# A layer norm moved from TensorE transposes to GpSimd with factors spread over DRAM, in a two-layer convolution and attention kernel

## The chip, the cores and the metric

The kernel runs on one core of a Trainium2 chip. The metric is the device time of one execution in microseconds. A time is given as the median of several executions; a profile is one execution, and its span is a few microseconds shorter than the time. The kernel before took 929.19 us.

Engines are named as in the profile: PE is TensorE's matmul, PEld its weight load, DVE VectorE, ACT ScalarE, POOL GpSimd, SP SyncE, which issues most DMAs.

## The reference, cut to what matters

Layer 0 normalises each pixel over its 128 channels, adds a depthwise 3x3 convolution, and attends inside 16x16 windows; layer 1 is linear attention and a recurrence over the tokens.

```python
def _layernorm2d(x, g, b):                    # x is (4, 128, 64, 64)
    mean = x.mean(axis=1, keepdims=True)      # over the 128 channels
    var = ((x - mean) ** 2).mean(axis=1, keepdims=True)
    return (x - mean) / jnp.sqrt(var + EPS) * g + b

y = _layernorm2d(x, ln_g, ln_b)
y = y + _cpe(y, cpe_w, cpe_b)                 # depthwise 3x3
q, k, v = 1x1 projections of y in 16x16 windows, 2 branches x 4 heads
o = softmax(q . 5x5 neighbours of k) applied to v     # zero padding counts in the sum
x = x + (Wo of o)
# layer 1: t = t + linear_attention(norm(t)); t = t + recurrence(norm(t))
```

## The kernel before

The image is cut into 16 bands of 16 rows, a band into 4 windows. The program is one long interleaving: while TensorE does window i's attention (six "gaps" a window), one step of `ahead` (norm and convolution of the next band) and one step of `behind` (layer 1 of the band before) are put into a gap. The program holds each engine of the list `ENGINES` to the order in which its instructions are written, so the place of a step decides what it waits behind. (The first window of a band takes steps of `ahead` in three of its gaps only, so a band has 3 + 3 x 6 = 21 of them.)

The norm needs sums over channels. The statistics are taken with tokens on the partitions, where one instruction sums over channels; the convolution wants channels on the partitions. So four pieces of 128 tokens are scaled on VectorE, turned by TensorE, and evicted by ScalarE into a padded image:

```python
def turn(g):
    j0, j1 = groups[g]
    rows = turned(xn.pop(g), 0, j1 - j0)[:, : (j1 - j0) * P]   # 4 PE transposes
    ...
    evict(y[:, 2 * j0 + 1 : k1, 1 : W + 1], rows[...])          # ACT, from PSUM
measure(0); yield; measure(1); yield; scale(0); yield
for g in range(len(groups)):
    turn(g); scale(g + 1); measure(g + 2); yield
...
def taps(y2, y, c0, width, each):
    for tap in range(9):
        src = y[:, dy : dy + WS, c0 + dx : c0 + dx + width]
        if tap == 0:
            nc.scalar.activation(y2, src, AF.Identity, bias=cpe_b, scale=cpe_w[:, 0:1])
        else:
            nc.vector.scalar_tensor_tensor(y2, src, cpe_w[:, tap : tap + 1], y2, ALU.mult, ALU.add)
        if tap % each == 0:
            yield
def convolve(n, half):             # half a band: two windows
    yield from taps(y2, y, half * 2 * WS, 2 * WS, 1 + half)
    nc.scalar.copy(y2w, y2)        # (views cut) the projections of two windows read y2w
```

A band has sixteen such taps on VectorE, eight for each half.

The sums of the softmax go ScalarE, DMA (`dc`), VectorE (inverses), DMA to DRAM (`rd`), DMA back to all partitions (`rden`), and GpSimd multiplies (`oT`). Layer 1's first matmuls of a band (line 471 before, 552 after) read `oT`; their starts serve below as the mile post of a band.

## Time and profile before

| | before |
|---|---|
| time, median | 929.19 us (928.76 to 930.86) |
| span of the profile | 925.6 us |
| mean granted clock | 0.981 |
| start to first line 471 | 77.57 us |
| first to second band | 50.16 us |
| 13 bands, from 127.73 to 779.47 us | 651.74 us, 50.13 each |
| last band to last product | 42.83 us |
| rest | 103.3 us |

The five stretches add up to the span. The row of the 13 steady bands is the one to watch; this is its line of busy times, with the columns that the prediction explains:

```profile
127.73:779.47 651.74, 648.91 (x8363) 495.55 (x8359) 550.74 (x1849) 406.12 (x739) 180.20 (x252) 1.00 0.19 55
```

TensorE is idle for 651.74 - 648.91 = 2.8 us in thirteen bands. Why that is so shows in how one half of the convolution is made (the timeline of the kernel before; columns: start, duration, engine, line, what, and in brackets the idle time before it, if any):

```profile
449.58 0.74 DVE L294 SCALAR_TENSOR_TENSOR y<-ypad,cpe_w,y 128x512 f32<-128x512 f32 x1
451.36 0.74 DVE L294 SCALAR_TENSOR_TENSOR y<-ypad,cpe_w,y 128x512 f32<-128x512 f32 x1
452.13 0.62 ACT L330 COPY y2w<-y 128x512 f32<-128x512 f32 x1
...
454.61 1.03 PE L343 MATMUL bank<-y2w,wqT 128*128 128x256 f32 x4
```

The eight taps of this half began at 437.73 us and came one or two at a time between VectorE's other work. The copy starts as the last tap ends, and the matmuls that read it start 2.5 us later: they do not wait. The list of waits (engine, line, the one waited for, us in total, times, longest) has the copies, and no matmul of line 343 behind a copy:

```profile
ACT y2w L330 <- DVE y L294: 17.5, 16, 5.8
```

### The profile page before, as it was taken

The numbers are of one execution on the slowest core, as the hardware profiler recorded it, in microseconds if no ns is written. First come the engines' busy times: TensorE is split into PE (matmuls) and PEld (weight loads), VectorE is DVE, ScalarE is ACT, GpSimd is POOL, SyncE is SP. The second block draws the span as 40 slices with busy tenths as digits, with TensorE's granted clock in tenths as the row PEclk, the third lists the DMA queues.
The fourth block names the chain that finished last, engine by engine and source line by source line (L and its number), as shares of the span: only waits on it lengthen the run. The fifth ranks groups of instructions, "written<-read, shape, count | busy, mean of one in ns | idle before, by whom it ended". The sixth has DMA issues, their size and how long they took to land.

```text
span 925.6 us, 26464 instructions
## 1 busy us (share of the span) xinstructions
PE 876.4 (95%) x10508; PEld 655.1 (71%) x10508; DVE 730.4 (79%) x2408; ACT 540.1 (58%) x1010; POOL 260.8 (28%) x358
## 2 busy tenths in 40 slices
PE   4978999999999999999999999999999999977894
PEld 3856777877777877777787777777777878665452
DVE  6464979888798878798888889787879887578684
ACT  3655656565756565665657575666666565623563
POOL 2122141423232232304132323323230412121195
PEclk9988999999999999999999999999999999989898
DMA  4112121122212121212112121212121111153254
GB/s 122 26 46 62 38 70 49 47 59 63 60 55 60 54 57 49 74 38 68 49 51 60 60 60 49 62 45 73 49 70 39 55 37 50 41 210 132 86 219 150
DMA packets 53189, 63.46 MB, mean 69 GB/s; under 512 B 22976, under 2 KB 33856, under 8 KB 52416
## 3 DMA queue, kind: packets, MB, share of 16 engines
q1 hardware_dynamic: 51616, 61.10, 21.1%
q8 instruction: 85, 1.39, 0.6%
q10 hardware_dynamic: 1440, 0.57, 0.2%
q14 instruction: 48, 0.39, 0.1%
HBM read 35.44 MB, written 17.30 MB: 57 GB/s over the span
## 4 chain that ended last, share of the span: by engine, by line
PE 61%; DVE 24%; ACT 5%; POOL 4%; issue 3%; DMA 2%; ACTq 0%; POOLq 0%; DVEq 0%; SPq 0%
PE bank L343 8%; DVE y L294 8%; PE bank L471 7%; PE bank L388 6%; PE bank L218 6%; PE bank L500 5%; PE bank L406 4%; PE bank L356 4%; PE bank L418 4%; PE bank L608 3%; DVE st L197 2%; PE z L834 2%; PE bank L579 2%; PE bank L543 2%; PE bank L581 2%
## 5 line engine op out<-in xcount | busy, mean ns | idle before, releaser
L294 DVE SCALAR_TENSOR_TENSOR y<-ypad,cpe_w,y 128x512 f32<-128x512 f32 x240 | 189.8, 791 | 17.1 <-ACT y L292 13.6
L397 ACT ACTIVATE es<-bank 128x512 f32<-128x512 f32 x256 | 132.2, 602 | 77.0 <-PE bank L388 77.0
L446 POOL TENSOR_TENSOR oT<-o_sb,rden 128x512 f32<-128x512 f32 x64 | 83.9, 1311 | 242.7 <-DMA rden<-rd 138.4
L201 POOL TENSOR_SCALAR rs<-mv 128x4 f32<-128x4 f32 (+2 forms) x100 | 25.1, 251 | 366.5 <-DVE mv L199 163.2
L209 DVE TENSOR_SCALAR xn<-x,mv,rs 128x128 f32<-128x128 f32 x256 | 89.9, 412 | 26.6 <-POOL rs L202 26.6
L202 POOL TENSOR_TENSOR rs<-rs,mhalf 128x4 f32<-128x4 f32 (+2 forms) x100 | 106.3, 1063 | 8.3
L388 PEld LDWEIGHTS bank<-q,k 32*128 32x128 f32 x3072 | 97.7, 189 | 7.5 <-ACT k L351 6.3
L388 PE MATMUL bank<-q,k 32*128 32x96 f32 (+1 forms) x3072 | 96.3, 270 | 1.1 <-ACT k L351 1.1
L418 PEld LDWEIGHTS bank<-es,v_sb 128*32 128x32 f32 x3072 | 56.6, 110 | 30.2 <-issue 20.2
L471 PE MATMUL bank<-woT,oT 128*128 128x128 f32 x512 | 68.0, 289 | 5.8 <-POOL oT L446 5.8
L471 PEld LDWEIGHTS bank<-woT,oT 128*128 128x128 f32 x512 | 64.8, 202 | 9.9 <-POOL oT L446 7.5
L500 PE MATMUL bank<-xl,awT 128*128 128x512 f32 x128 | 70.0, 630 | 0.0
L418 PE MATMUL bank<-es,v_sb 128*32 128x96 f32 (+1 forms) x3072 | 69.9, 239 | 0.0
L406 PE MATMUL bank<-es,ones 128*32 128x512 f32 x512 | 69.1, 612 | 0.0
L363 ACT COPY v_sb<-bank 128x512 f32<-128x512 f32 x64 | 37.6, 587 | 53.6 <-PE bank L356 44.6
L343 PE MATMUL bank<-y2w,wqT 128*128 128x256 f32 x256 | 67.3, 386 | 1.0 <-DVE y2w L294 1.0
L343 PE MATMUL bank<-y2w,wkT 128*128 128x256 f32 x256 | 66.7, 384 | 0.0
L356 PE MATMUL bank<-wvT,y2w 128*128 128x256 f32 x256 | 66.0, 380 | 0.0
L351 ACT COPY q<-bank 128x512 f32<-128x512 f32 x64 | 37.7, 588 | 42.2 <-PE bank L343 40.2
L351 ACT COPY k<-bank 128x512 f32<-128x512 f32 x64 | 37.4, 584 | 37.6 <-PE bank L343 37.5
L197 DVE BATCH_NORM_STATS2 st<-x 128x6 f32<-128x128 f32 x256 | 55.5, 280 | 1.1
L343 PEld LDWEIGHTS bank<-y2w,wqT 128*128 128x128 f32 x256 | 46.0, 195 | 13.0 <-issue 7.2
(118 smaller groups left out, 1713.7 us busy)
## 6 DMA issues: line engine op xcount, KB each, us to landing
rden<-rd SPq DMA_DIRECT2D x64, 256.0 KB
v_sb<-v_sb SPq DMA_DIRECT2D x128, 64.0 KB
resd<-rs_o SPq DMA_DIRECT2D x32, 256.0 KB
out<-ot SPq DMA_DIRECT2D x32, 256.0 KB
xin<-in_xt SPq DMA_DIRECT2D x15, 512.0 KB
res<-resd SPq DMA_DIRECT2D x3, 2048.0 KB
late<-resd SPq DMA_DIRECT2D x2, 1024.0 KB
dc<-den SPq DMA_DIRECT2D x64, 8.0 KB
```

Source lines behind the costliest of these rows:

```text
L202: nc.gpsimd.tensor_tensor(rs[:, :n], rs[:, :n], mhalf[:, :n], ALU.pow)
L209: nc.vector.tensor_scalar(xn[:, j, :], piece, mv[:, j, 0:1], rs[:, j : j + 1], ALU.subtract, ALU.mult)
L294: nc.vector.scalar_tensor_tensor(y2, src, cpe_w[:, tap : tap + 1], y2, ALU.mult, ALU.add)
L343: nc.tensor.matmul(pps[:, br * WT : (br + 1) * WT], wT[:, br * P : (br + 1) * P], y2, start=True, stop=True,)
L356: nc.tensor.matmul(vps[:, e * 256 : (e + 1) * 256], y2[:, e * P : (e + 1) * P], wvT, start=True, stop=True,)
L388: nc.tensor.matmul(sps[h][:, cols], w["k"][rows, k0 : k0 + P], w["q"][rows, cols], start=False, stop=(br, n) == pieces[-1],)
L397: nc.scalar.activation(es, sps[h], AF.Exp, scale=scale)
L406: nc.tensor.matmul(dps[rows], ones[:, :HD], w["es", h], start=True, stop=True)
L418: nc.tensor.matmul(ops[rows, cols], w["v"][:, n, c0 : c0 + HD], w["es", h][:, cols], start=(br, n) == pieces[0], stop=(br, n) == pieces[-1],)
L446: nc.gpsimd.tensor_tensor(oTs[n][:, :, :, wj * WS : (wj + 1) * WS], w["o"].rearrange("p (a r c) -> p a r c", a=BR, c=WS), w["rden"].rearra ...
L471: nc.tensor.matmul(yps[:, j * P : (j + 1) * P], oT[:, br, t], woT[:, br, :], start=br == 0, stop=br == BR - 1,)
L500: nc.tensor.matmul(zps, awT[:, m * P : (m + 1) * P], h.xl, start=True, stop=True)
```

## The change

Its intent is to take the norm's transposes off TensorE and the scaling off VectorE. The statistics stay as they are, but the two factors of each token (the inverse deviation, and the mean times it) go to DRAM and come back spread over all 128 partitions. A second copy of x, already with channels on the partitions and its tokens interleaved by piece, is loaded, and GpSimd multiplies and subtracts. The rest is a new table of steps, the sums moved into the slot of their logits, and SP's DMA issues held to the order of the source. To make room, `y2`, `q`, `k` and `o_sb` have one buffer instead of two.

```diff
-ENGINES = [... ("PE", "DVE", "Activation", "Pool")]
+ENGINES = [... ("PE", "DVE", "Activation", "Pool", "SP")]
+    class Group:
+        def measure(self):  # statistics as before, and nc.sync.dma_start(self.x, ins["xc"] ...)
+        def send(self):
+            self.there = dram4.tile([2, P, self.k], F32, ...)
+            nc.sync.dma_start(self.there.rearrange("f p j -> p f j"), self.both[:, :, : self.k])
+        def spread(self):
+            nc.sync.dma_start(self.all[:, :, : self.k * P],
+                self.there.rearrange("f p j -> f (p j)").partition_broadcast(P))
+        def scale(self):
+            nc.gpsimd.tensor_tensor(x, x, self.all[:, 0, : self.k * P], ALU.mult)
+            nc.gpsimd.tensor_tensor(x, x, self.all[:, 1, : self.k * P], ALU.subtract)
+        def evict(self):
+            x = self.x[:, : self.k * P].rearrange("c (r w j) -> c j r w", r=2, w=W)
+            # nc.scalar.activation into ypad, as before but from SBUF
... (front(): the generator is replaced by a table)
+            cuts = [(0, 4), (4, 8), (8, 9)] if wi == 0 else [(1, 5), (5, NCH + (wi < NB - 1))]
+            for e, (j0, j1) in enumerate(cuts):
+                g = Group(n, j0, j1)
+                at(k0 - 1 + e, g.measure)
+                at(k0 + 1 + e, g.send)
+                at(k0 + 3 + e, g.spread)
+                at(k0 + 6 + min(e, 1), g.scale)
+                at(k0 + 8 + min(e, 1), g.evict)
+            at(k0 + 9, edges, n)
+            for half, ks in enumerate((
+                    (10, 10, 11, 12, 13, 14, 15, 15, 16, 16),
+                    (17, 17, 18, 19, 19, 22, 23, 24, 25, 25))):
+                for e, k in enumerate(ks):
+                    at((k0 if half == 0 else k1) + k, tap_of, n, half, e)
... (main loop)
+        if after:
+            to_rows(windows[i - 1])          # rd back to all partitions
+        if inside and wj == 2:
+            load(n + 2)                      # and the head
         if inside:
+            sums(windows[i])                 # before: one slot later, in weighted()
...
+        if inside:
+            inverses(windows[i])             # in the same slot
... (a ring of 6 buffers in the recurrence; the last accumulation of an image is left out)
```

A band has 21 steps. The ten entries of a row `ks` are ScalarE's tap 0, eight VectorE taps, and the copy to `y2w`.

## The prediction

> **What bounds the kernel now.** I read the page first (busy shares and the 40 slices), then busy time by stretches, then the groups by shape, the order of time of one steady band, and last the start and the end of the layer loop, where the slices dip.
>
> ```profile
> PE 876.4 (95%) x10508; PEld 655.1 (71%) x10508; DVE 730.4 (79%) x2408; ACT 540.1 (58%) x1010; POOL 260.8 (28%) x358
> PE   4978999999999999999999999999999999977894
> PEclk9988999999999999999999999999999999989898
> ```
>
> TensorE is full nearly everywhere. The dips are slices 3 and 4 (46 to 93 us), where the granted clock falls too, and everything after about 810 us. The stretches say the same; the columns are length, then busy time with instructions of PE, PEld, DVE, ACT, POOL, then clock, DMA share and GB/s.
>
> ```profile
> 60.00:110.00 50.00, 42.31 (x519) 31.73 (x517) 34.38 (x100) 26.44 (x49) 12.24 (x15) 0.86 0.17 49
> ...
> 410.00:460.00 50.00, 49.79 (x640) 37.81 (x636) 43.01 (x144) 31.16 (x57) 14.28 (x19) 1.00 0.20 57
> ...
> 610.00:660.00 50.00, 49.98 (x645) 38.08 (x644) 42.26 (x145) 31.34 (x57) 13.74 (x19) 1.00 0.20 57
> ```
>
> In the steady part PE has no idle time, DVE is at 85%, ACT at 63%, POOL at 28%. A full PE row is not PE at its peak, so I checked its waits between 76 and 819 us: all waits of its matmuls on other engines come to under 8 us. The first layer-1 matmuls of a band (line 471) start at 127.73 us and, thirteen bands later, at 779.47 us: 651.74 / 13 = 50.1 us a band. That band is a queue of PE work. What leaves PE's queue is saved; what leaves DVE or ACT is not, unless they come to stall PE.
>
> **What the change takes from that queue** are the norm's transposes of bands 1 to 15:
>
> ```profile
> L209 DVE TENSOR_SCALAR xf<-xin,mv,rs 128x128 f32<-128x128 f32 x116 | 32.1, 338 | 1.4 <-POOL rs L202 1.3
> L218 PE MATMUL bank<-ident,xf 128*128 128x128 f32 x128 | 22.4, 296 | 9.8 <-DVE xf L209 9.7
> L446 POOL TENSOR_TENSOR oT<-o_sb,rden 128x512 f32<-128x512 f32 x64 | 83.9, 1311 | 242.7 <-DMA rden<-rd 138.4
> ```
>
> The 296 ns is one transpose with its latency, not its price. The price is how much later the next group starts (start, duration, engine, line, what):
>
> ```profile
> 425.44 0.60 PE L218 MATMUL bank<-ident,xf 128*128 128x128 f32 x4
> 425.97 1.06 PE L406 MATMUL bank<-es,ones 128*32 128x512 f32 x8
> 426.97 1.12 PE L608 MATMUL bank<-xl,fwT 128*128 128x512 f32 x2
> 427.93 0.60 PE L218 MATMUL bank<-ident,xf 128*128 128x128 f32 x4
> 428.46 1.09 PE L418 MATMUL bank<-es,v_sb 128*32 128x96 f32 x48
> ```
>
> Both groups of four hold the queue 0.53 us, 0.1325 us a transpose.
>
> **What the Trainium skill says.** (1) "TensorE: Matmul & The Clock Gate", Part 4: PE-mode transpose, gives about 275 ns in a kernel's context, output to PSUM. The trace agrees on the duration (296 ns) and shows the queue price as less than half. Its Part 1 says that the array runs at half rate after an idle window of about 3.4 us until it has been busy as long; the trace agrees: after the PE stall of 4.03 us at 61 us, 48 logit matmuls take 2.89 us instead of 1.48. (2) "SBUF — State Buffer", Who interferes with whom: a DVE instruction with two SBUF inputs, or in a 2-port mode, is blocked for the whole of a GpSimd instruction that reads SBUF. The trace agrees: beside the GpSimd product at 404.43 us two taps of the convolution take 2.40 us together instead of 1.53 as two others do at 408.03, while a DVE read of PSUM beside another product (aT at 417.66) keeps its 0.66 us. (3) "GPSIMD Engine Reference", section 3.1, gives 2.6 cycles an element for a two-input operation: 512 x 2.6 / 1.2 GHz = 1.11 us plus dispatch; the trace has 1.28 us (median). (4) "DMA: Bandwidth & Descriptors", Two DMAs through the same engine are not ordered: a DMA that reads what another wrote has to wait on its semaphore before it is issued. So each hop over DRAM is a full landing, and with SP now held to source order such a wait also holds up every later DMA.
>
> **The change part by part.**
>
> Removed. Bands 1 to 15 have 3 x 9 + 4 x 8 + 4 x 8 + 4 x 7 = 119 transposes. I count band 1's eight in the start below; the other 111 x 0.1325 us = 14.7 us off PE's queue, 1.06 us of each 50.1 us band. DVE loses 119 scalings, 1.11 us per group of four, 33 us in all. ACT's eviction remains, now from SBUF; it costs the same (0.82 us from PSUM; line 292, which reads SBUF, 0.81 us for the same size).
>
> Added. Per full group: one small GpSimd product (about 0.25 us, like the 128x4 scalar operation of line 201) and two of 128x512, 2 x 1.28 us; two groups a band make 5.6 us. POOL goes from 13.7 to about 19.3 us a band of 49: not the bound. DVE is blocked by them only where it runs taps, xn, low or the inverses. In the new table of steps the taps of a band's halves lie at steps k0+10 to 16 and k0+17 to 25, which is k0-4 to k0+4 of the next band; the scalings sit at k0+6 and k0+7, in the hole. So I charge DVE about 1 us a band against 2.2 us saved. DMA gets 2 x (256 + 512) KB more a band on top of 57 GB/s x 50 us = 2.8 MB: about 88 GB/s, off every path if it lands in time. A step is 50.1 / 21 = 2.39 us. The nearest transfer to compare is rden, 256 KB spread over 128 partitions: issued at 44.06, used at 49.30, so 5.2 us. The 512 KB spread I estimate at 7 us, just the three steps before the scaling, with two more before the eviction by ACT. The small store has two steps, 4.8 us. Enough, without much over.
>
> Moved. The sums of a window go into its own slot, behind about 4 us of other PE work, when its exponentials (2.07 us) are done, so no new PE wait. Dividing by them comes a slot earlier, so oT is ready before layer 1 asks for it.
>
> The start. In the flow, line 471 follows the band's logits by 6.2 us (423.31 to 429.48). Here slot 5 begins at 60.86, so it should start at 67.0:
>
> ```profile
> 60.86 0.39 PE L383 MATMUL bank<-mask_q,mask_k 32*128 32x512 bf16 x3
> 65.27 0.58 PE L383 MATMUL bank<-mask_q,mask_k 32*128 32x512 bf16 x1 [4.03 <-ACT den L409]
> 66.74 2.89 PE L388 MATMUL bank<-q,k 32*128 32x96 f32 x48 [0.89 <-ACT k L351]
> ...
> 77.57 3.57 PE L471 MATMUL bank<-woT,oT 128*128 128x128 f32 x16 [2.77 <-POOL oT L446]
> ```
>
> 10.5 us late, and 1.5 us more in those 16 matmuls at the low clock: 12 us lost. Six taps in a row on DVE held up ACT's ordered queue, that held up PE, and then oT waited for rden. The new table spreads these taps and has oT early, so the hole closes. But band 1's norm now takes two hops in slots of only 6.4 us: factors at about 27 us, stored by 29, spreads issued only behind the sums' DMA (about 31.6) and landed near 39 and 42, scaled by 45. ACT's eviction then holds up PE in slot 1 by about 6 us, with perhaps 1.5 us of low clock. Net 12 - 7.5 = 4.5 us.
>
> The tail. After the last window PE waits for the last product:
>
> ```profile
> 820.98 1.26 POOL L446 TENSOR_TENSOR oT<-o_sb,rden 128x512 f32<-128x512 f32 x1
> 822.30 3.79 PE L471 MATMUL bank<-woT,oT 128*128 128x128 f32 x16 [2.47 <-POOL oT L446]
> ```
>
> rden was issued at 815.37; it will be some 7 us earlier. That saves the wait of 2.5 us, and about 1 us of DVE's xn beside that product (2.05 us instead of 1.11): 3.5 us.
>
> The rest. The deeper ring frees ACT in the counted rounds, but each round lasts 1.22 us because GpSimd adds the residual for 1.10 us and the final check comes after the last sum: nothing, or half a microsecond. The skipped accumulation, and the short oT waits at other band starts, 1 us.
>
> Sum: 14.7 + 4.5 + 3.5 + 1.0 = 23.7 us, so 905.5. DVE's lower load might mend some small PE waits on DVE, 3 to 4 us between 76 and 819 us; I take 1.5 us: **904 us**, 0.973 of before.
>
> **The rivals.**
>
> A. GpSimd blocks DVE enough to stall PE. For it: DVE is already at 85% and a 2.6 us pair of scalings can stop xn or a low. If each of the 33 groups cost PE 0.5 us more, the steady gain would be gone: about 920. Against: taps are kept out of that window, DVE gives up 33 us, and PE hardly waits for DVE now although 64 such products run already.
>
> B. SP in source order. One late store stops the spreads, then v and the input loads behind it. For it: SP already waits 50.6 us for rd to land before rden. Against: every dependent pair is one to three steps apart. If a wait of 1 us reached PE in each slot, 64 us would come on top; a slip at band starts alone (15 x 1 us) gives 919.
>
> C. The start goes better than I think: the sends beat the sums' DMA and the whole 12 us is recovered. Then with all else 896 to 898.
>
> D. PE was not the bound, and nothing is saved by fewer transposes. Only start and tail would count: 919. Against: the back-to-back starts above.
>
> **Range and chances.** PE's share is nearly arithmetic, the start is worth 0 to 12 us, contention 0 to 15. That gives 890 to 914 for 8 in 10. The 2% line is 910.6 us, about 7 us above my figure: faster 0.78, within 2% 0.20, slower 0.02.
>
> **What would show it.** Right: L218 with xf falls from 128 to 9 transposes; line 471 comes every 49.0 us; two GpSimd groups of 128x512 with about 60 products in sum at 1.3 us; PE still free of waits in the steady part; line 471 first near 71 to 73 us; no wait of PE on POOL in the tail. Wrong: a band of 50 us or more with PE waiting on ACT (an eviction held by a spread) or on DVE, long SP waits before the spreads, or a first band that begins as late as before.

## More of the kernel before

`y2w` is the tile to keep in mind: the first matmuls of a window's projections (line 343 before, 418 after) wait for its copy (line 330 before, 405 after), which waits for the eighth tap (line 294 before, 369 after).

## The result, and the profile after

The kernel after took 987.82 us (median of 4 runs, 986.78 to 988.29) beside 930.03 for the kernel before on the same chip: the ratio is 1.0613, with a 95% interval of 1.058 to 1.0646. It is correct, and it is slower by 6%. (A ratio is the mean time of one kernel's fast runs over that of the other's of the same rounds, so it is not quite the ratio of the medians quoted.)

The page of the profile after, busy time and two rows of the slices:

```profile
span 984.7 us, 26419 instructions
PE 884.5 (90%) x10380; PEld 652.0 (66%) x10381; DVE 736.4 (75%) x2285; ACT 551.3 (56%) x1018; POOL 337.4 (34%) x457
PE   4988898989989898989999898979899899998795
```

TensorE has 128 instructions fewer and yet 8 us more busy time, and its row has eights all along, where there were nines. The two steady stretches that the prediction showed are no longer full, and the clock is down:

```profile
410.00:460.00 50.00, 44.87 (x522) 33.81 (x522) 37.05 (x115) 29.40 (x52) 18.57 (x26) 0.97 0.34 80
610.00:660.00 50.00, 44.19 (x550) 32.18 (x549) 36.51 (x126) 27.88 (x51) 19.56 (x30) 0.97 0.37 90
```

| | before | after | difference |
|---|---|---|---|
| start to the first line 471 (552) | 77.57 | 76.43 | -1.1 |
| first to second band | 50.16 | 55.68 | +5.5 |
| 13 bands | 651.74 | 710.29 | +58.5 |
| last band to last product | 42.83 | 39.95 | -2.9 |
| rest | 103.3 | 102.35 | -0.95 |
| span | 925.6 | 984.7 | +59.1 |

So the whole loss lies in the steady bands. Their line of busy times, after:

```profile
132.11:842.40 710.29, 658.60 (x8261) 498.26 (x8257) 559.99 (x1750) 415.93 (x748) 246.84 (x338) 0.97 0.30 79
```

TensorE is now idle for 710.29 - 658.60 = 51.7 us instead of 2.8, and its clock is 0.97 instead of 1.00. What it waits for, in the list of waits:

```profile
ACT y2w L405 <- DVE y L369: 91.5, 30, 6.3
PEld bank L418 <- ACT y2w L405: 68.6, 28, 4.3
DVE dc L491 <- DMA dc<-den: 46.0, 17, 6.7
PE bank L418 <- ACT y2w L405: 43.4, 24, 3.4
PE bank L226 <- DVE xn L217: 13.5, 12, 2.5
```

The chain is whole in these lines: the projections wait for the copy to `y2w`, and all thirty copies wait for the last tap. In the kernel before, 16 copies waited, 17.5 us in sum, and no matmul behind them. (Of the 46.0 us for `dc`, 19 lie before the first band.) One such place, in the timeline after:

```profile
482.56 0.74 DVE L369 SCALAR_TENSOR_TENSOR y<-ypad,cpe_w,y 128x512 f32<-128x512 f32 x1
...
490.39 1.53 DVE L369 SCALAR_TENSOR_TENSOR y<-ypad,cpe_w,y 128x512 f32<-128x512 f32 x2
...
492.96 0.74 DVE L369 SCALAR_TENSOR_TENSOR y<-ypad,cpe_w,y 128x512 f32<-128x512 f32 x1
493.74 0.62 ACT L405 COPY y2w<-y 128x512 f32<-128x512 f32 x1 [3.64 <-DVE y L369]
...
494.41 1.34 PE L418 MATMUL bank<-y2w,wqT 128*128 128x256 f32 x4 [2.43 <-ACT y2w L405]
...
495.55 1.91 PE L598 MATMUL bank<-awT,xl 128*128 128x128 f32 x8
```

The first tap of this half starts at 482.56 us, just after the evicted edges and ScalarE's tap 0. From 481.42 to 493.70 us VectorE has no gap: beside the eight taps this stretch holds four `low` and `f` pairs (the first just before the first tap), `v`, `aT` and the four small operations of the inverses. The eight taps get 11.1 us from first start to last end, against 14.4 us before. TensorE stands for 2.43 us, and the next eight matmuls take 1.91 us, where the same eight took 1.05 us at 482.21 us. There are fourteen such waits at line 418, of 2.15 to 3.42 us, between 108 and 819 us, and ten of them are followed by matmuls at about half speed. This costs twice. VectorE loses by it too: ScalarE, held up at the late copy, comes to tap 0 of the second half only at 495.22 us, and VectorE stands for 2.37 us before its next tap. VectorE has 16 waits for such a tap 0, 47.1 us in all (13.3 of them one wait at the start), against 2 and 13.6 us in the kernel before and 2 and 13.7 us in e5.

The groups by shape, for the prices:

```profile
L217 DVE TENSOR_SCALAR xn<-x,mv,rs 128x128 f32<-128x128 f32 x256 | 119.3, 528 | 43.4 <-POOL rs L207 43.4
L292 POOL TENSOR_TENSOR xf<-xf,all 128x512 f32<-128x512 f32 x26 | 33.4, 1283 | 21.0 <-DMA all<-both_d 21.0
L299 ACT ACTIVATE ypad<-xf,ln_b,ln_g 128x512 f32<-128x512 f32 x18 | 23.7, 1315 | 10.5 <-POOL xf L293 10.4
L226 PE MATMUL bank<-ident,xf 128*128 128x128 f32 x9 | 3.0, 468 | 10.0 <-DVE xf L217 9.8
```

The transposes fell from 128 to 9, and GpSimd's operation costs 1.28 us. ScalarE's eviction costs 1.315 us, not 0.82. Layer 1's scaling `xn` costs 528 ns a piece, where it cost 412 before. (It is only present in this list as a mean; one group of four that ran beside a pair of scalings took 3.17 us instead of 1.11.)

### The profile page after: what moved, and what is told of

The parts are those of the page before. It is cut to its first block, busy times and chain, and to the rows that moved or that the text cites.

```text
span 984.7 us, 26419 instructions
## 1 busy us (share of the span) xinstructions
PE 884.5 (90%) x10380; PEld 652.0 (66%) x10381; DVE 736.4 (75%) x2285; ACT 551.3 (56%) x1018; POOL 337.4 (34%) x457
## 4 chain that ended last, share of the span: by engine, by line
DVE 35%; PE 32%; DMA 11%; ACT 8%; POOL 8%; issue 4%; SPq 1%; ACTq 0%; POOLq 0%; DVEq 0%
DVE y L369 8%; DVE xn L217 7%; PE bank L418 6%; DMA dc<-den 5%; PE z L951 4%; POOL rs L207 3%; DVE f L586 3%; DVE st L198 3%; DMA all<-both_d 3%; PE bank L463 3%; PE bank L642 2%; PE bank L480 2%; PE bank L598 2%; ACT ypad L299 2%; PE bank L661 2%
## 5 line engine op out<-in xcount | busy, mean ns | idle before, releaser
L369 DVE SCALAR_TENSOR_TENSOR y<-ypad,cpe_w,y 128x512 f32<-128x512 f32 x240 | 189.7, 791 | 49.8 <-ACT y L367 47.1
L217 DVE TENSOR_SCALAR xn<-x,mv,rs 128x128 f32<-128x128 f32 x256 | 119.3, 528 | 43.4 <-POOL rs L207 43.4
L418 PE MATMUL bank<-y2w,wqT 128*128 128x256 f32 x256 | 74.3, 414 | 44.6 <-ACT y2w L405 43.4
L206 POOL TENSOR_SCALAR rs<-mv 128x4 f32<-128x4 f32 (+1 forms) x67 | 18.7, 279 | 209.6 <-DVE mv L200 189.0
L480 PE MATMUL bank<-es,ones 128*32 128x512 f32 x512 | 75.8, 612 | 0.7 <-ACT es L472 0.7
L418 PE MATMUL bank<-y2w,wkT 128*128 128x256 f32 x256 | 73.6, 414 | 0.0
L552 PE MATMUL bank<-woT,oT 128*128 128x128 f32 x512 | 65.6, 283 | 5.5 <-POOL oT L527 5.5
L405 ACT COPY y2w<-y 128x512 f32<-128x512 f32 x30 | 18.5, 618 | 91.5 <-DVE y L369 91.5
L207 POOL TENSOR_TENSOR rs<-rs,mhalf 128x4 f32<-128x4 f32 (+1 forms) x67 | 67.1, 1001 | 5.6
L552 PEld LDWEIGHTS bank<-woT,oT 128*128 128x128 f32 x512 | 62.6, 196 | 9.0 <-POOL oT L527 6.1
L226 PE MATMUL bank<-ident,xn 128*128 128x128 f32 x256 | 49.1, 290 | 13.6 <-DVE xn L217 13.5
```

The lines of the kernel that those rows point to most:

```text
L207: nc.gpsimd.tensor_tensor(rs[:, :n], rs[:, :n], mhalf[:, :n], ALU.pow)
L217: nc.vector.tensor_scalar(xn[:, j, :], piece, mv[:, j, 0:1], rs[:, j : j + 1], ALU.subtract, ALU.mult)
L418: nc.tensor.matmul(pps[:, br * WT : (br + 1) * WT], wT[:, br * P : (br + 1) * P], y2, start=True, stop=True,)
L480: nc.tensor.matmul(dps[rows], ones[:, :HD], w["es", h], start=True, stop=True)
L552: nc.tensor.matmul(yps[:, j * P : (j + 1) * P], oT[:, br, t], woT[:, br, :], start=br == 0, stop=br == BR - 1,)
```

## The experiments

Eighteen kernels were run. All are correct unless it is said that they are wrong. Ratios are to the kernel before in the same rounds. The expectations are quoted; some use short names for theories. The text after each says in full what was meant. These are the theories that were in play:

- **Taps too late** (theories T and R in the texts): norm and convolution of a band lie so that the sixteen taps end after the copy is wanted.
- **Late landings** (theory D): small DMAs (`dc`, `rd`) land late behind large ones, and what waits on them holds up VectorE.
- **GpSimd blocks VectorE** (theory G): the two operations of 1.28 us keep VectorE from SBUF.
- **SP's order** (theory S): a DMA waiting at SP's head holds up those behind it.
- **The one-piece group** (theory F in the texts): bands 4, 8 and 12 have a third group of a single piece, whose trip over DRAM holds up others.

### First four: which part of the change costs

**e1**, the taps of the first half packed two a step, so that the copy comes two steps sooner:

```diff
-                    (10, 10, 11, 12, 13, 14, 15, 15, 16, 16),
+                    (10, 10, 11, 11, 12, 12, 13, 13, 14, 14),
```

> The changed kernel with one thing altered: the ten calls of each band's first convolution half come at steps 10,10,11,11,12,12,13,13,14,14 instead of 10,10,11,12,13,14,15,15,16,16. Theory T (the table puts the copy of the first half into the very slot that uses it, so any lag of VectorE reaches TensorE; the profile after has 15 waits of TensorE's projections on that copy of 2.2 to 3.4 us, each followed by some half-clock): these waits vanish, 935 to 945 us. Theory D (VectorE is held by late landings of the sums' store and stays late whatever the table says): the waits shrink by no more than a third, 970 to 985 us. Theory G (GpSimd blocks VectorE so that it has too little capacity): the wait reappears elsewhere, 975 us or more.

Measured: 999.85 us, ratio 1.0773 (1.0717 to 1.083), worse than after. The waits of e1 on VectorE and behind it:

```profile
PE bank L616 <- DVE f L586: 20.6, 14, 1.9
PE bank L480 <- ACT es L472: 16.7, 15, 1.1
```

The wait at line 418 is nearly gone (7.2 us are left of 43.4), but layer 1's `f` and the exponentials now wait for VectorE and ScalarE. Theories T and D missed; what theory G forecast (the wait reappears elsewhere, 975 us or more) came, but it does not show that GpSimd is the reason. What follows is that the work was not merely in the wrong order: in this stretch VectorE has more to do than fits, and whoever comes last waits.

**e2**, the 512 KB load and the head moved behind the inverses of the third window:

```diff
-        if inside and wj == 2:              # between gaps 0 and 1
-            load_head(n + 3); load(n + 2)
...
+        if inside and wj == 2:              # after inverses(windows[i])
+            load_head(n + 3); load(n + 2)
```

> The changed kernel with the load of the next band's 512 KB (and of its head) moved from before the sums of the third window to after its inverses, so that in SP's source order it stands behind the small sums' transfer. Theory D (that load lies ahead of the sums' transfer in the queue, the transfer then lands 4.5 to 5 us after issue, VectorE stands at the addition of the sums and is late with the last taps): the third window's landing falls to 2 to 3 us and half or more of the projection waits goes, 950 to 965 us. Theory T (only the table is late): less than 10 us gained, 978 to 988 us. Theory S (source order of the queue in general): also little, 980 us or more.

Measured: 972.0 us, ratio 1.0477 (1.0442 to 1.0512). VectorE's waits for `dc` fell from 46.0 to 34.7 us; those at line 418 only from 43.4 to 38.8 us. The time lies between the ranges of theories D and T. Late landings are real, and worth 13 to 16 us, but not the main cause.

**e3**, SP left out of the source order (the one word removed from `ENGINES`):

> The changed kernel with SP taken out of the engines that are held to source order; all four compute engines keep their order to the instruction. Theory S (source order on the queue blocks small transfers behind waits for big ones, such as the spread that waited 8 us for its store): 940 to 955 us. Theory T or G: within 10 us of the changed kernel, 978 to 998 us, since nothing on the compute engines changes. It could also get slower, if the scheduler's own order puts the spreads still earlier.

Measured: 1057.51 us, ratio 1.1402 (1.1363 to 1.1442). VectorE's waits for `dc` doubled:

```profile
DVE dc L491 <- DMA dc<-den: 96.3, 18, 12.3
```

SP's order is not the culprit. With this many dependent transfers it helps by some 70 us, and the order that the compiler chose is worse.

**e4**, norm and convolution as before (the generator, the transposes), all the rest as after:

```diff
-            ... (the table of steps)
+            yield from norm_rows(n)
+            if bands[n][1]:
+                yield
+            yield from convolve(n, 0)
+            yield
+            ... (as before)
```

> The changed kernel with the front end of before (norm through TensorE transposes, scaled on VectorE, taps in the old steps); sums in their slot, SP in source order, the earlier products and the longer ring stay. If the new front is to blame (table T or GpSimd G): 915 to 928 us, a little below before by the earlier products at start and tail. If the sums in their own slot or the queue order are to blame (D or S): 955 us or more.

Measured: 938.37 us beside 928.17, ratio 1.0107 (1.008 to 1.0134). This splits the loss: the rest of the change, which I had put down as a gain of some microseconds, costs 10 us by itself; the new norm and its table cost the other 49 us (987.8 - 938.4). (The run also gives `y2` its second buffer back. Neither range expected was met.) Where the 10 us sit can be read from the waits of e4: its transposes of layer 1 wait for the residual `x` of line 675 in 16 places, 15.5 us in all; in the kernel before that was 3.1 us.

### The table of steps

**e5**, the norm of bands 2 to 15 four steps earlier, and the taps one a step from there:

```diff
+            ke = k0 if n == 1 else k0 - 4
-                at(k0 - 1 + e, g.measure)       # and send, spread, scale, evict, edges
+                at(ke - 1 + e, g.measure)
-                    (10, 10, 11, 12, 13, 14, 15, 15, 16, 16),
-                    (17, 17, 18, 19, 19, 22, 23, 24, 25, 25),
+                    (6, 7, 8, 9, 10, 11, 12, 13, 14, 15),         # band 1 unchanged
+                    (17, 17, 18, 19, 19, 21, 22, 23, 24, 24),
```

> The changed kernel with the whole norm of bands 2 to 15 (measuring, store, spread, scaling, eviction, edges) four steps earlier, and the first half's ten calls at steps 6 to 15, one a step, as in the kernel before; the second half ends one step sooner. No operation is added or removed. Theory R (the round trip over DRAM takes the first ten steps of the band, so VectorE gets its sixteen taps only in the steps where layer 1 loads it most; e1 showed that moving the taps alone moves the wait): the projections' waits on the copy fall from 25 to few, and the time to 930 to 950 us. Theory G (GpSimd's added products take VectorE's time wherever they stand): 970 us or more. Theory D (late landings of the sums): 965 to 980 us, with VectorE's waits on that transfer unchanged.

Measured: 932.5 us, ratio 1.0045 (1.0007 to 1.0082): of the loss, 55 of 58 us are gone (53 by the ratios), and every instruction of the new norm is still there. The timeline of e5 at the same work:

```profile
462.11 0.74 DVE L369 SCALAR_TENSOR_TENSOR y<-ypad,cpe_w,y 128x512 f32<-128x512 f32 x1
463.13 0.64 ACT L405 COPY y2w<-y 128x512 f32<-128x512 f32 x1
...
465.67 1.13 PE L418 MATMUL bank<-y2w,wqT 128*128 128x256 f32 x4
```

The copy is again 2.5 us ahead of its readers, as in the kernel before, and the list of waits no longer has line 418 waiting for it; of the thirty copies, ten wait:

```profile
ACT y2w L405 <- DVE y L369: 12.4, 10, 8.5
```

The taps are not cheaper (867 ns on average, 791 in the kernel after), and `xn` still costs 477 ns: VectorE may be as slow as that, if its work is at the right time.

**e15**, the norm four steps earlier, the taps left as after (the first three lines of e5's diff only):

> The fourth corner with the changed kernel, e1_taps0 and e5_shift: the norm of bands 2 to 15 four steps earlier, but the taps at the steps of the changed kernel. Theory R (the taps have too few steps between the eviction and the copy, and taps and norm must move together): little gained, 970 to 985 us, waits on the copy still there. Theory L (the late eviction alone, and GpSimd's scalings colliding with xn in front of the taps, is what makes VectorE late; the table of taps is good enough): 930 to 945 us, like e5_shift, with the waits on the copy gone.

Measured: 989.66 us, ratio 1.0653 (1.0624 to 1.0681): no gain, and line 418 waits 49.8 us. So it is not the factors' arrival that held up the taps. With e1 and e5 there are four tables: neither moved 988, taps packed 1000, norm alone 990, norm earlier and taps spread 932.5. (They are not a clean square: e1 packs the taps and e5 spreads them, and taps spread without the earlier norm cannot be run, since the image is not there yet.) Only both together helped; as I read it, because the room that the earlier norm makes has to be used to spread the taps over the steps before the deadline.

### Late landings, once the taps are right

**e6**, e5 with the loads at the end of the second window's slot:

```diff
-        if inside and wj == 2:              # e5: between gaps 0 and 1
+        if inside and wj == 1:              # after inverses(windows[i])
```

> e5_shift, and the 512 KB load moved to the end of the second window's slot, behind the sums' transfer. Theory D adds to R: another 10 to 20 us off e5_shift, since e2 got 16 us from moving the load alone. If R holds alone: within 5 us of e5_shift.

Measured: 933.24 us, ratio 1.008 (1.0039 to 1.012): no gain over e5, as expected if the place of the taps holds alone. What e2 had won was won on the badly timed kernel; here it lies beside other work. The gains overlap and must not be added.

**e7**, e6 with the inverses in the slot after:

```diff
         if after:
+            inverses(windows[i - 1])
             to_rows(windows[i - 1])
...
-        if inside:
-            inverses(windows[i])
```

> e6_shift_load1, and the inverses of the sums issued on VectorE one gap later, in the next slot, when their transfer has landed. Theory D: VectorE's waits on the sums' transfer (46 us in the changed kernel) fall under 10 us and the time by another 5 to 15 us; the products on GpSimd come later, which costs nothing as long as layer 1 does not wait for them. If nothing hangs on these waits any more: within 5 us of e6_shift_load1. If R and D both hold and TensorE is the bound again, 905 to 920 us, which would beat the kernel before.

Measured: 926.6 us, ratio 0.9998 (0.9964 to 1.0032), 6.6 us better than e6. VectorE's waits for `dc`, which were to fall under 10 us, hardly changed (36.0 to 35.8 us). What changed is what stands behind them: in e5 and e6 TensorE waited three times, 4.5 to 5.4 us each in e5 (180, 385 and 589 us), for the residual `x` behind such a wait, and these waits for `x` fell from 16.7 to 0.8 us. TensorE now waits in few places; the largest are four waits for `oT` at a band's start, 16.0 us together. At one of them `rd` had taken 8 us to land (issued at 567.63, read at 576.04 us).

**e9**, the kernel after with the spreads issued by ScalarE's queue instead of SP's:

```diff
-            nc.sync.dma_start(
+            nc.scalar.dma_start(
                 self.all[:, :, : self.k * P],
```

> The changed kernel with one thing altered: the 512 KB spreads of the factors are issued from ACT's queue instead of SP's. Theory D in its sharper form (small transfers, the sums, the inverses and the 4-byte store, wait in SP's ring behind 512 KB spreads; in e7_inv_next 8 KB of inverses took 8 us to land behind two of them): VectorE's waits on the sums fall from 46 us to 25 us or less, 965 to 978 us. If the ring does not matter[...]: 982 to 992 us. If the waits of the issue on ACT hurt its ordered queue: slower, 990 to 1000 us.

Measured: 988.04 us, ratio 1.0603 (1.0559 to 1.0648): no difference from after.

**e10**, e7 with that same edit:

> e7_inv_next with the spreads issued from ACT's queue. Theory D in its sharper form: the waits of TensorE on GpSimd's products at the batches' starts (16.0 us in e7_inv_next, four times) fall to 10 us or less, 912 to 920 us. If the ring does not matter: 924 to 929 us.

Measured: 926.04 us, ratio 0.995 (0.9914 to 0.9986), half a per cent better than e7 by the ratios and the same by the medians; the intervals overlap, so it is not clear of noise, and it lies where it was expected if the queue does not matter. The ordinary bands now take 48.3 to 49.2 us; the three in which the first band of a new image (4, 8 and 12) is normed take 52 to 53, the band after each takes 50.6, and each of the three is followed by one wait of 3.0 to 3.3 us for `oT`.

**e11**, e10 with the inverses of the first five windows in their own slot, for the start:

```diff
-            inverses(windows[i - 1])
+            if i > 5:
+                inverses(windows[i - 1])
...
+        if inside and i < 5:
+            inverses(windows[i])
```

> e10_e7_spread_act with the inverses of the first five windows back in their own slot, since those slots last only 6 to 8 us and the products came late there (TensorE waited 8.35 us at 83 us in e7_inv_next). If the start is limited by that: line 552 first before 77 us and 5 to 9 us off e10_e7_spread_act. If it is limited by band 1's own round trip: within 2 us of it.

Measured: 929.0 us, ratio 0.9971 (0.9935 to 1.0007): no gain. Line 552 first comes at 80.82 us, as in e10 (80.64). Why the start did not profit was not settled.

**e12**, e4 (the norm of before) with e7's move of the inverses:

> e4_old_front (norm on TensorE as before) with the inverses in the next slot. It tells what the norm on GpSimd is worth once nothing else differs. If e4's 10 us over before came from VectorE standing at the sums' transfer: 922 to 930 us. If the norm itself saves TensorE the 14.7 us I predicted, the versions e7 or e10 with the new norm lie 8 us or more below this run; if the gain is used up elsewhere (VectorE blocked by GpSimd, DMA), they lie within 5 us of it or above.

Measured: 945.24 us, ratio 1.0152 (1.0099 to 1.0205), worse than e4's 938.37. A miss: the move that helped the new norm does harm beside the old one. The waits show where: VectorE's for `dc` rise from 17.6 to 30.6 us, and TensorE's for the residual `x` from 15.5 to 22.7 us; why `dc` is waited for longer was not looked into. By the ratios e7 and e10 are 14 to 19 us faster than this run, but they also load the bands at another place, so this is no clean price of the norm.

### GpSimd beside VectorE

**e8**, wrong: the kernel after, but GpSimd scales only as many columns as there are pieces, so its two operations are nearly free.

```diff
-            x = self.x[:, : self.k * P]
-            nc.gpsimd.tensor_tensor(x, x, self.all[:, 0, : self.k * P], ALU.mult)
+            x = self.x[:, : self.k]
+            nc.gpsimd.tensor_tensor(x, x, self.all[:, 0, : self.k], ALU.mult)
```

> Wrong result on purpose: the changed kernel, but GpSimd's two operations work on the first four columns of a group only, so each takes about 0.2 us instead of 1.28 us; all transfers, waits and the order stay. Theory G (GpSimd's reads block VectorE's two-input and 2-port instructions): 940 to 955 us, with xn back from 0.53 to about 0.4 us. Theory R (the place of the taps): 975 to 985 us; about 2.6 us a group comes off the chain before the eviction, and little else changes.

Measured: 954.73 us, ratio 1.0289 (1.0253 to 1.0324), some 30 us better than after. VectorE's busy time falls by 34.8 us (736.4 to 701.6), and `xn` from 528 to 374 ns. The waits at line 418 are still 33.2 us. So the blocking costs VectorE about 35 us of its time, and on a kernel where VectorE is late nearly all of it reaches the end. (The edit also brings the eviction some 2 us earlier; by e15 an eviction four steps earlier gains nothing.)

**e14**, wrong: the same edit on e10.

> Wrong result on purpose: e10_e7_spread_act with GpSimd's two operations on four columns a group only. In e8_tiny_scale the same edit took 33 us off the badly timed kernel. If GpSimd's work costs as such (VectorE short of time wherever it stands): 895 to 908 us. If it costs only where VectorE is late already (the badly timed kernel): within 6 us of e10, 920 to 926 us.

Measured: 919.39 us, ratio 0.9919 (0.9889 to 0.9948). That is 3 us below e10 by the ratios, whose intervals overlap, and 7 by the medians, although VectorE's busy time is again much lower (699.1 us). The same blocking that cost 30 us costs at most some 3 to 7 us where the taps have room.

### The one-piece group

In e10 the wait at a band's start comes from two small stores that land late. The timeline of e10 (rows of SPq and ACTq are DMA issues), and the line of busy times of 3 us in between:

```profile
362.51 0.53 SPq L279 DMA_DIRECT2D both_d<-both  x1
...
371.55 0.33 ACTq L285 DMA_DIRECT2D all<-both_d  x1
...
372.26 0.58 SPq L502 DMA_DIRECT2D rden<-rd  x1
...
381.13 2.05 PE L552 MATMUL bank<-woT,oT 128*128 128x128 f32 x16 [3.31 <-POOL oT L527]
```

```profile
368.00:371.00 3.00, 3.00 (x23) 2.85 (x23) 2.35 (x7) 0.00 (x0) 2.52 (x3) 1.00 0.12 4
```

The store of the one-piece group is issued at 362.51 us; what reads it can be issued only at 371.55, and ScalarE, whose queue holds that issue, does nothing from 368 to 371 us. `rd`, issued by the same queue at 364.56, is read at 372.26. In those 3 us the DMA engines are 12% busy, so by then it is not bandwidth that either store waits for. The one-piece store is 256 pieces of 4 bytes; those of four pieces, whose runs are 16 bytes, were read within 4.3 us (issued at 357.62, spread issued at 361.95).

**e13**, e10 with the third group's spread and scaling two steps later:

```diff
+                last = e == 2
-                at(ke + 3 + e, g.spread)
+                at(ke + 3 + e + 2 * last, g.spread)      # and scale likewise
```

> e10_e7_spread_act with the spread and scaling of the third, one-piece group of each batch's first band two steps later. In e10 the bands before a batch take about 53 us against 48.3 to 49.6 us for others, with TensorE waiting 3.0 to 3.3 us for a product of GpSimd. If the third group's own hops block there: these three waits vanish, 6 to 12 us off. If it is the sum of transfers or of VectorE's extra work in such a band: within 3 us of e10.

Measured: 936.68 us, ratio 1.0079 (1.0035 to 1.0123), worse than e10 by some 11 us. A miss. The trace shows one cost of it: the eviction was not moved along, and ScalarE, in order, stands three times, 11.9 us in all, for the late scaling of the short group; TensorE's waits for `oT` fell only from 9.6 to 6.3 us. Whether that is all of the 11 us was not tested.

**e16**, e10 with the one-piece group scaled by VectorE and turned by one TensorE transpose, as in the kernel before, without store and spread:

```diff
         def spread(self):
+            if self.small: return                        # send likewise
         def scale(self):
+            if self.small:
+                nc.vector.tensor_scalar(self.x, piece, mv[:, 0, 0:1], rs[:, 0:1],
+                                        ALU.subtract, ALU.mult)
+                return
         def evict(self):
+            if self.small:
+                tps = bank()
+                nc.tensor.transpose(tps[:, :P], self.x, ident)
+                ... (two evictions from PSUM)
```

> e10_e7_spread_act with the one-piece third group of the bands 4, 8 and 12 taken back to the old way: scaled on VectorE, turned by one transpose on TensorE, no store, no spread. Its store writes 256 elements of 4 bytes, and in e10 the 8 KB of inverses issued behind it landed only after 7.7 us with the transfer engines nearly idle for the last 3 us. Theory F (that store of 4-byte elements is slow and holds the queue): TensorE's three waits of 3.0 to 3.3 us on GpSimd's product at the batches' starts vanish, 912 to 920 us. If it is only the sum of transfers in such a band: 922 to 928 us.

Measured over 5 rounds: 907.82 us, ratio 0.9772 (0.9743 to 0.9801). It beats both kernels, the one before by 2.3% (whether by more than 2% is unclear). The thirteen bands of e16:

```profile
130.13:763.93 633.80, 633.25 (x8263) 483.92 (x8259) 553.45 (x1752) 417.43 (x747) 262.58 (x327) 1.00 0.29 86
```

TensorE is idle for 0.55 us in 634, and a band takes 633.80 / 13 = 48.75 us. That three short groups cost e10 some 16 to 18 us is shown; that the 4-byte pieces are the reason is argued from the stretch above and was not tested by itself.

**e17**, the same edit on the kernel after:

> The changed kernel with only that third group taken back. SP stood up to 8.0 us, three times, at the spread behind that store. Theory F: 8 to 20 us off the changed kernel, 968 to 980 us, while the waits on the copy of the first half stay. If the store does not matter: 984 to 990 us.

Measured: 973.82 us, ratio 1.0508 (1.0467 to 1.0549), 10 to 14 us better than after, with 41.0 us of waits left at line 418. So this cost was in the change as written, but it was not the main one.

**e18**, the same edit on e7, so with the spreads on SP's queue:

> e7_inv_next (spreads on SP's queue) with only that third group taken back. Theory F: 912 to 920 us, like e16; if the spreads themselves delay small transfers in SP's ring, it stays 3 us or more above e16.

Measured over 5 rounds: 911.75 us, ratio 0.9828 (0.98 to 0.9857). The gain over e7 is 15 us, like that over e10; the spreads' queue may be worth half a per cent, as between e7 and e10; here too the intervals overlap.

## Why the prediction was right or wrong

The prediction said 904 us and faster with a chance of 0.78; it was 988 us, outside the range and slower, to which it gave 0.02. **The step that failed** is in "Added": "the taps of a band's halves lie at steps k0+10 to 16 and k0+17 to 25 ... the scalings sit at k0+6 and k0+7, in the hole". It took the five steps without taps (k0+5 to k0+9) as a shelter from GpSimd, and never asked what waiting for the norm does to the taps. The trip over DRAM fills a band's first ten steps, the eight taps of the first half then have seven steps (10 to 16), these lie where layer 1 gives VectorE its `low`, `f`, `v` and `aT`, and the copy at step 16 is read in the same slot. In the kernel before the taps came one a step from k0+6, with the copy at k0+15. The "What leaves PE's queue is saved; what leaves DVE or ACT is not, unless they come to stall PE" of its first part was right, and its last clause is what happened.

The thirteen bands give the sum, with the measured lines in place of the prediction's terms. e16 has nearly the same TensorE instructions as after (8263 and 8261) with hardly a wait and at full clock, so its busy time shows what this work costs unhindered:

| term, thirteen bands | us |
|---|---|
| TensorE work removed: 633.25 - 648.91 | -15.66 |
| the same work, busy for longer: 658.60 - 633.25 | +25.35 |
| more idle time: 51.69 - 2.83 | +48.86 |
| sum, which is 710.29 - 651.74 | +58.55 |

Point by point:

- **The transposes.** Right: 128 became 9, and the TensorE work removed is 15.7 us in thirteen bands, where 13 x 1.06 = 13.8 us were predicted (the skipped accumulations are in the measured figure). It was lost more than four times over.
- **"PE still free of waits in the steady part".** Wrong, for the reason above; shown by e5, which moves only steps and takes back 53 to 55 of the 58 us; e15 (norm alone) and e1 (taps alone, packed) gain nothing.
- **Half clock.** The prediction knew of it (its point 1 of the skill) but had no term for it in the steady bands. The three groups of matmuls after the wait at 494 us took 1.7 us more than the same groups after the wait at 602 us, which was followed by full speed; nine of the ten such cases lie in the thirteen bands and make an estimated 15 of the table's 25 us. The rest I did not trace.
- **GpSimd beside VectorE (rival A).** The mechanism was right and the size off: "I charge DVE about 1 us a band against 2.2 us saved". VectorE's busy time in thirteen bands rose by 9.25 us, 0.7 a band, where it should have fallen by 1.2: the charge was 2.9 us. The scalings were kept away from the taps, but `xn` of layer 1 was not (528 ns for 412). What this is worth depends on the table: 30 us on the kernel after (e8), at most 3 to 7 us on e10 (e14). So on the kernel as written rival A came true, at twice its 16 us; once the taps have room it is less than that. The gains of e5 and e8 overlap and must not be added.
- **"ACT's eviction ... costs the same".** Off: 1.315 us instead of 0.82. My comparison was an activation that reads SBUF along rows (0.81 us); this one reads every fourth element, since the pieces are interleaved. The Trainium skill says as much in "Advanced Engine Details and Errata", SBUF Cachelines: full speed when accesses that follow one another fall in the same 16 bytes, a penalty when each falls in another. Four fp32 elements are 16 bytes, so the trace agrees, and I had not looked. The same line has the control: 128x128 elements take 607 ns out of groups interleaved by four, and 484 ns out of the one-piece group, which is not interleaved. It adds about 1 us a band to ScalarE, which is not the bound; no run shows what it alone costs.
- **Landings.** "The 512 KB spread I estimate at 7 us ... Enough, without much over" was about right for the spreads (13 waits of GpSimd, 21.0 us in all, and in e15 no gain from their being sent earlier). What was missed is what they and the loads do to the small transfers: VectorE waits 46.0 us for `dc` (e2: 13 to 16 us), and the one-piece group's store (e17: 10 to 14 us). "Dividing by them comes a slot earlier, so oT is ready before layer 1 asks for it" overlooked that `dc` must then land within its own slot, and VectorE stands in order behind it; that this is a part of the 10 us of e4 (17.6 us of waits for `dc`, 7.1 before) is argued, not tested.
- **SP in source order (rival B).** It does no harm; without it the kernel is 70 us slower (e3).
- **The start.** Predicted 4.5 us, measured 1.1 us, and then 5.5 us lost in the first band. In e16 the first layer-1 matmul even comes at 82.93 us, 5.4 later than before, and the first band takes back 3.0. What holds up the start was not settled; e11 did not mend it.
- **The tail.** Right: 2.9 us of the predicted 3.5, and no matmul there waits for GpSimd. **The rest**: 0.95 us, predicted as nothing or half a microsecond in the recurrence.
- **POOL and DMA loads.** Right: "19.3 us a band", measured 246.84 / 13 = 19.0; "about 88 GB/s", measured 79 in the thirteen bands, 86 in e16. (The 1.11 us of its third point on the skill is an estimate from the page's cycles and clock; the trace has 1.28.)

The last line of the working is of interest with e16 in view: 49.0 us a band was predicted, and e16 has 48.75, with two groups a band still on GpSimd: the gain expected in the steady bands was there to be had. That e16 takes 907.8 us where 904 was predicted is partly luck: it is another kernel, with five edits; its thirteen bands gain 17.9 us, where 49.0 us a band would give 14.7, and its start with the first band loses 2.4 us, where 4.5 were to be gained. What lost the gain was the table of steps above all, then where the loads and the inverses stand, and a group too small for the trip.

## What to carry to other kernels

When an operation is replaced by one that is cheaper but takes longer from start to end, work out the latest step at which its reader can still be on time, and count what the engine in between has to do from there to the deadline; an engine with a middling average has full stretches (VectorE after the change: 79% busy in the thirteen bands, and no gap from 481.42 to 493.70 us). Judge a new mechanism only after its table of steps has been moved with it: here packing the taps or moving the norm alone gained nothing, and both together gained 55 us. And take out of a bulk path the piece that is too small for it.

## What the Trainium skill lacked or had wrong

- "TensorE: Matmul & The Clock Gate", Part 1 and "Why this matters for your kernels": the page asks for an idle window of about 3.4 us, and its rule for kernels is no gap above some 3 us. Here ten of fourteen waits of 2.15 to 3.42 us were followed by about half rate (eight matmuls 1.91 us instead of 1.05), the shortest after 2.15 and 2.35 us, while waits of 2.42, 2.66, 2.77 and 2.78 us, and one of 3.31 us in e10, were not. The page's free-running window may explain why like waits differ, but not that one shorter than the window was enough; the rule for kernels is too generous.
- The same page, Part 4: PE-mode transpose, has the duration (275 ns; 296 here) and not the price in a full queue, 0.53 us for four in the kernel before.
- "Advanced Engine Details and Errata", SBUF Cachelines, is right and gives no size: a ScalarE activation of 128x512 that reads every fourth fp32 element took 1.315 us, one that reads SBUF along rows 0.817 us; of 128x128 on the same line, 607 and 484 ns.
- "DMA: Bandwidth & Descriptors" does not say how late a small store can land behind large transfers: 1 KB in pieces of 4 bytes 9.0 us to the issue of its reader and 8 KB behind it 7.7 us, at a DMA share of 0.12 near the end. Its section Issuing engines are not separate DMA queues held: another issuing engine changed nothing in e9, and in e10 half a per cent, which is not clear of noise.
- "SBUF — State Buffer", Who interferes with whom, has the rule and was right. No page says what it costs a whole kernel, which is no property of the instructions: the same scalings cost 30 us in one table of steps and at most 3 to 7 us in another.
